# Weighting a pair's sums out of PSUM and adding the six statistics by one matmul in a four-layer graph kernel

## The chip, the cores and the metric

The kernel runs on one core of a Trainium2 chip. The core's engines are TensorE (PE; its weight loads are listed as PEld), VectorE (DVE), ScalarE (ACT), GpSimd (POOL) and SyncE (SP). Here SP issues the transfers between device memory and the on-chip memory SBUF. Matmuls write into PSUM, a small memory of eight banks that VectorE and ScalarE read. The metric is the device time of one execution, in microseconds.

## The reference, cut to what matters

Four graph layers follow each other on 16 graphs of 1024 nodes with 64 channels. The input is x (16, 1024, 64), a 0/1 adjacency adj (16, 1024, 1024) and a node mask. Between the layers stands `x = layernorm(x + layer(x))`. The change touches the first layer. It thins out the neighbours of each node and then takes, for every node and channel, a weighted sum of three quantiles over the values of the node's remaining neighbours:

```python
for tau, wt in zip([0.25, 0.5, 0.75], [0.25, 0.5, 0.25]):
    pos = clip(tau * (mf - 1.0), 0.0)          # mf: number of neighbours left
    lo, hi = floor(pos), ceil(pos)
    frac = pos - lo
    q = gather(lo) * (1 - frac) + gather(hi) * frac   # lo-th and hi-th smallest value
    agg = agg + wt * q
out = x + agg
y = relu(out @ W1 + b1) @ W2 + b2
```

So for each node and channel six values are wanted, the value at `lo` and at `hi` for three quantiles. These are the six statistics (S = 6 in the kernel). Each is multiplied by a weight that depends on the node and the statistic alone (wt times frac or 1 - frac), and the six products are added. Layers 2, 3 and 4 multiply by the adjacency or its transpose: layer 2 three times by adj, layer 3 once by the transposed adjacency with a degree norm, layer 4 once more by it.

## The kernel before, in words

**Steps, units and pairs.** The values of a channel are sorted once. Then for each node the wanted rank is found by counting. Work is cut into units: a graph g, a group gr of eight channels (G8 = 8) and a half h of the nodes (HALF = 512). A unit has six steps, one for each statistic. Two units with the same g and gr, the two halves, make a pair. That gives 96 steps and eight pairs per graph, 128 pairs in all, and 1536 steps. One loop (L1365) runs over the steps y. In each turn it issues, with lags, the parts of several steps at once:

- VectorE: `masks` (L636) of step y+1 and `products` (L644) of step y. A product is written into one of two buffers of the pool `prod`.
- TensorE and ScalarE: `words` (L654) of step y-2 reads a product buffer by matmuls into a bank named pw, and ScalarE copies it out. `ranks` (L666) runs for step y-3 and `steps` (L674) for step y-4. The last ends with the values `val` of a statistic, 8 channels by 512 nodes spread over 128 partitions.
- `Sums.add` (L692) adds `val` of four steps at a time into one PSUM bank, `fc`. After three such adds the bank holds the whole pair: 12 rows of 8 channels, one for each half and statistic, at the partitions that `row_of` (L684) names, by 512 nodes.
- `Sums.store` (L701) runs one turn after the third add: ScalarE copies `fc` into SBUF and SP stores all 128 partitions, 256 KB, to `aggd` in device memory.

TensorE also runs the counting matmuls of the next units (`counts`, L596) and turns the words of the next group into matmul weights (`word_part`, L550). These use two PSUM banks of the tag "y" in turn (`side_bank`, L97): pa, y0, y1 and pw. The weights lie in a pool `wts` of five buffers, two for a group.

**The background.** Beside the steps run generators: the sort of the values for two graphs, the thinning of the next graph's adjacency (`dilate`), the degrees, and the layers of the graph before (`layers`, L830). `Spread` (L977) decides at which half step each generator takes its next step, from a number of steps that is given to it (69 for the layers), a first and a last place, and two running estimates of VectorE's and TensorE's load. Sort steps are fillers: they take places where VectorE's estimate is not ahead. The sorts, the thinning and the degrees are over before the last graphs, which have the steps and the layers alone.

**The order.** `link` (L137) ties the instructions of TensorE, and inside the loop those of VectorE and ScalarE, to the order in which the program issues them. SP's transfers have no such tie and are placed by the framework's scheduler. The SP queue works in order, and each of its transfers can wait for tiles to come free.

**The layers of a graph.** `layers` begins by loading x, the mask, the weights `wd` of the six statistics spread over the channels (three tiles of 128x1024 in 16 bits, six transfers) and the sums from `aggd` (three tiles of 128x1024, twelve transfers). Then VectorE multiplies the three tiles by their weights, adds the three products, and adds the two halves of the result into `pre` (L867 to L875). After that `pre` is scaled, x is added, and the first layer's two matmuls (`ph`, `py`) follow.

**The end.** After the last step only the layers of the last graph are left, one after another. For them `held` (L804) reuses the buffers of the step loop (five of `wts`, two of `cc`, four half buffers of `dw`, four of `prod`, one of `mt`) to hold the whole adjacency and its transpose of the last graph, 16 tiles of 512 KB. It issues the loads in one loop. `stay_warm` (L712) puts matmuls without use into TensorE's order in this part: 72 between the start of the layers and the first `ph`, fewer later.

Of the kernel before, what the change touches and what calls it, by code (L numbers as in the profile page):

```python
# [9 lines left out]
F32 = mybir.dt.float32  # L10
# [9 lines left out]
P = 128  # L20
# [13 lines left out]
S = 6  # L34
# [8 lines left out]
def gnn_stack(  # L43
# [35 lines left out]
    wts = ctx.enter_context(tc.tile_pool(name="wts", bufs=5))  # L79
# [607 lines left out]
    class Sums:  # L687
# [12 lines left out]

        def store(self):  # L701
            v = work.tile([P, HALF], F32, tag="sv", name="v", bufs=1)
            A.copy(v, self.fc)
            nc.sync.dma_start(out=self.gi["aggd"][self.gr], in_=v)
# [99 lines left out]
    def held(g):  # L804

        tiles = []
        for i in range(5):
            t = wts.tile([P, 2, T, P], F16, tag="xw", name="xw").rearrange("p x t m -> p (x t m)")
            tiles.append(t.bitcast(F32))
# [11 lines left out]
        for i in range(1):  # L821
            t = big.tile([P, KC, HALF], F16, tag="mt", name="mt", bufs=6).rearrange("p k n -> p (k n)")
            tiles.append(t.bitcast(F32))
        for j in range(2 * T):
            nc.sync.dma_start(
                out=tiles[j], in_=adj[g, ts(j, P), :] if j < T else adjT[g, ts(j - T, P), :]
            )
        return tiles[0:T], tiles[T : 2 * T]

    def layers(g, aggd, wd, least, den, deg, rows=(), columns=()):  # L830
# [14 lines left out]
        terms, weights = [], []  # L845
        for i in range(S // 2):
            w = wide("w", tag=("hT", "hw", "node")[i]).bitcast(F16)
            w = w.rearrange("p (s n) -> p s n", s=2)
            halves_in(
                w, lambda h: wd[ds(2 * i, 2), ts(h, HALF)].partition_broadcast(C)  # L850
            )
            weights.append(w)
        for i in range(S // 2):
            a = strm.tile([P, N], F32, tag="a", name="v").rearrange("p (s n) -> p s n", s=2)
            for s_ in range(2):
                halves_in(a[:, s_], lambda h: aggd[:, ds(row_of(S * h + 2 * i + s_), G8)])
            terms.append(a)
# [9 lines left out]
        for a, w in zip(terms, weights):  # L867
            yield
            V.tensor_tensor(a, a, w, ALU.mult)
        for a in terms[1:]:  # L870
            yield
            V.tensor_tensor(terms[0], terms[0], a, ALU.add)
        yield
        pre = wide("pre", tag="yT")
        V.tensor_tensor(pre, terms[0][:, 0], terms[0][:, 1], ALU.add)  # L875
# [173 lines left out]
    def info(g):  # L1049
# [14 lines left out]
        nc.sync.dma_start(out=rcs[g % 2][0:S], in_=rd)  # L1064
        infos[g].update(least=least, txw=txw)
# [131 lines left out]


# [306 lines left out]
```

## Time and profile before

| what | value |
|---|---|
| median of 3 runs | 8277.14 us (8274.99 to 8284.68) |
| profiled execution, its own time | 8271.02 us |
| its span in the profile | 8269.2 us |
| first product of the step loop starts at | 297.8 us |
| last product starts at | 8129.1 us |
| one graph of 96 steps | 443 to 513 us |

The profile gives for each engine its busy time and its number of instructions. Groups of instructions are listed by line, engine, operation and tile, with the shape written as partitions x elements, the count, the busy time in us and the mean length in ns. Behind the second bar stands the idle time of the engine just before them and who ended it. A line L176 is the helper that records VectorE's and ScalarE's operations, and L156 the one for matmuls, so the groups are told apart by their tiles: `pr<-mt,dw` is a product, `pw<-pr,red` the matmuls that read it, `fc<-val,fin` the adds, `v<-fc` the copy of `store`, `v<-v,w` the weighting in the layers. A float32 matmul shows as two rows, one for each pass. In the lists of waits a line names the waiting engine and tile, then who ended the wait, and then the total in us, the number of times and the longest. In a timeline the first column is the start and the second the length, both in us. A table by stretch has the stretch and its length, then the busy time and count of PE, PEld, DVE, ACT and POOL, then the granted TensorE clock, the share of the DMA engines and GB/s.

### The profile page before, as it was taken

What the parts mean: (1) busy time and instruction counts of PE and PEld (TensorE: products, weight loads), DVE (VectorE), ACT (ScalarE), POOL (GpSimd) and SP (SyncE); (2) the same over time, 40 slices, a digit from 0 to 9 for tenths busy, and PEclk for the clock granted to TensorE, in tenths of its full rate; (3) what the DMA queues carried; (4) which work ended last, traced back from release to release, by engine and by line L of the source; (5) the groups of instructions that cost most, each with busy time, mean ns of one, the idle gap of its engine ahead of it and who ended that gap; (6) DMA issues with size and microseconds to landing.
All of it is one profiled execution on the core that took longest, in us unless ns stands there. A gap on an engine that the chain in (4) does not pass through costs nothing. (4 is left out here: it accounts for less than half of the span.)

```text
span 8269.2 us, 164242 instructions
## 1 busy us (share of the span) xinstructions
PE 7311.8 (88%) x65169; PEld 2994.8 (36%) x65169; DVE 7826.2 (95%) x8924; ACT 7060.5 (85%) x13562; POOL 1321.6 (16%) x942
## 2 busy tenths in 40 slices
PE   0688889999999899898899999999899999999997
PEld 0233333333333333333333333333333333334333
DVE  9899999999999999999999999999999999887874
ACT  1689889888898889989898898988989888899993
POOL 2210202112021110202112021210202112020000
PEclk9999999999999999999999999999999999999999
DMA  3212222232223232232233322233222233222222
GB/s 101 48 42 53 94 88 93 79 101 98 88 86 87 86 104 91 90 93 90 80 99 104 81 93 89 80 100 94 91 94 85 85 97 104 72 89 72 65 88 68
DMA packets 530453, 711.85 MB, mean 86 GB/s; under 512 B 201488, under 2 KB 328848, under 8 KB 529680
## 3 DMA queue, kind: packets, MB, share of 16 engines
q1 hardware_dynamic: 529680, 701.34, 27.3%
q8 instruction: 510, 8.36, 0.4%
q14 instruction: 263, 2.15, 0.1%
HBM read 602.38 MB, written 98.77 MB: 85 GB/s over the span
## 5 line engine op out<-in xcount | busy, mean ns | idle before, releaser
L176 DVE TENSOR_TENSOR pr<-mt,dw 128x4096 f16<-128x4096 f16 x1536 | 3507.8, 2284 | 222.7 <-PE pw L156 166.7
L156 PE MATMUL x<-vt,xw 128*128 128x512 f16 x8192 | 2317.9, 386 | 0.0
L176 DVE TENSOR_TENSOR mt<-cc,rB 128x2048 f16<-128x2048 f16 x1536 | 1864.7, 1214 | 15.4 <-ACT cc L176 15.4
L176 ACT ACTIVATE pv<-pv,col 128x512 f32<-128x512 f32 x1536 | 1077.1, 701 | 0.0
L156 PEld LDWEIGHTS <-xw 128*128 128x128 f16 x8192 | 737.8, 99 | 819.9 <-issue 298.3
L176 ACT ACTIVATE qq<-pw 128x512 f16<-128x512 f32 x1536 | 962.1, 626 | 16.5 <-PE pw L156 15.9
L156 PE MATMUL pv<-mt,txw 128*32 128x512 f16 x12288 | 951.6, 387 | 8.6 <-ACT pv L176 8.6
L176 ACT ACTIVATE val<-pv 128x512 f32<-128x512 f32 x1536 | 948.9, 618 | 9.2 <-PE pv L156 8.9
L156 PE MATMUL pw<-pr,red 128*32 128x512 f16 x12288 | 937.7, 381 | 14.7 <-DVE pr L176 14.7
L176 ACT ACTIVATE pa<-pa,col 128x512 f32<-128x512 f32 x1020 | 712.5, 699 | 224.8 <-PE pa L156 223.2
L176 ACT ACTIVATE dw<-y 128x512 f16<-128x512 f32 x1024 | 636.9, 622 | 261.2 <-PE y L156 238.7
L734 POOL TENSOR_TENSOR rstd<-var,neghalf 128x8 f32<-128x8 f32 x112 | 250.0, 2232 | 3473.9 <-DVE var L176 3473.9
L176 ACT ACTIVATE cc<-x 128x512 f16<-128x512 f32 x1024 | 620.9, 606 | 190.2 <-PE x L156 112.8
L176 ACT ACTIVATE xw<-pa,col 128x512 f16<-128x512 f32 x1020 | 700.8, 687 | 33.0
L176 ACT ACTIVATE dw<-y,col 128x512 f16<-128x512 f32 x1024 | 719.2, 702 | 1.6 <-PE pv L156 1.1
L156 PE MATMUL pw<-ranks,subr 128*32 128x512 f16 x6144 | 603.0, 382 | 66.5 <-ACT xw L176 64.1
L176 ACT ACTIVATE h<-x 128x512 f16<-128x512 f32 x1024 | 640.0, 625 | 1.0 <-PE x L156 1.0
L176 ACT ACTIVATE l<-x 128x512 f16<-128x512 f32 x1024 | 604.0, 590 | 9.4 <-PE x L156 9.2
L156 PE MATMUL pv<-qq,lead 128*32 128x512 f16 x6144 | 603.6, 381 | 0.0
L156 PE MATMUL x<-h,neg 128*128 128x512 f16 x1024 | 393.9, 385 | 225.3 <-ACT h L176 206.4
L156 PEld LDWEIGHTS <-txw 128*32 128x32 f16 x12288 | 186.3, 94 | 1051.0 <-issue 1050.3
L176 DVE TENSOR_TENSOR sr<-sr 128x384 f16<-128x384 f16 (+9 forms) x1328 | 546.4, 441 | 17.7
(226 smaller groups left out, 10547.6 us busy)
## 6 DMA issues: line engine op xcount, KB each, us to landing
a<-adj_dram SPq DMA_DIRECT2D x360, 512.0 KB
a<-adjT_dram SPq DMA_DIRECT2D x240, 512.0 KB
da<-adj_dram SPq DMA_DIRECT2D x256, 256.0 KB
ac<-adjT_dram SPq DMA_DIRECT2D x256, 256.0 KB
aggd<-v SPq DMA_DIRECT2D x128, 256.0 KB
rB<-rn SPq DMA_DIRECT2D x96, 256.0 KB
v<-aggd SPq DMA_DIRECT2D x192, 128.0 KB
w<-wd SPq DMA_DIRECT2D x96, 128.0 KB
```

The lines of the kernel that those rows point to most:

```text
L156: link("PE", nc.tensor.matmul(out, **kw))
L176: ins = call(*args, **kw)
L734: nc.gpsimd.tensor_tensor(rstd, var, neghalf, ALU.pow)
```

## The change

There are two parts.

**The sums of a pair.** A pair's bank `fc` is no longer copied by ScalarE and stored whole. `weigh` runs on VectorE at the turn where `store` ran: it multiplies the bank by a tile `wf` that holds, at the same partitions, each statistic's weights for the 512 nodes of its half, and writes 128x512 float32 into SBUF. One turn later `store` issues one float32 matmul with a constant 0/1 matrix `choose` (128x32) which adds the six statistics of each half and channel; the result, two blocks of 8 channels, lies in a bank `pu` of the tag "y". ScalarE copies its 32 partitions, and SP stores the two blocks of 16 KB. The two `wf` tiles serve even and odd graphs. They are cleared once, and filled by twelve small transfers per graph at step S+2 of the graph. In `layers` the six weight loads, the twelve loads of sums, the three products and the three sums go; two loads bring `pre`. The layers have 65 steps in `Spread` instead of 69.

**The last graph's adjacency.** `held` takes four buffers of `wts` and two of `mt`, and the pool `wts` has four buffers. It issues the eight loads of the adjacency. The eight of the transposed adjacency are issued by a function that `layers` calls after its load of `pre`.

```diff
-    wts = ctx.enter_context(tc.tile_pool(name="wts", bufs=5))
+    wts = ctx.enter_context(tc.tile_pool(name="wts", bufs=4))
...
+        def weigh(self):
+            self.v = work.tile([P, HALF], F32, tag="sv", name="v", bufs=1)
+            V.tensor_tensor(self.v, self.fc, wfs[self.gi["g"] % 2], ALU.mult)
+
         def store(self):
-            v = work.tile([P, HALF], F32, tag="sv", name="v", bufs=1)
-            A.copy(v, self.fc)
-            nc.sync.dma_start(out=self.gi["aggd"][self.gr], in_=v)
+            pu = side_bank("pu")
+            mm(pu[0:32], choose, self.v, True, True, 0)
+            of = work.tile([32, HALF], F32, tag="of", name="of", bufs=1)
+            A.copy(of, pu[0:32])
+            for h in range(2):
+                nc.sync.dma_start(
+                    out=self.gi["aggd"][h, ds(G8 * self.gr, G8)], in_=of[ds(G8 * h, G8)]
+                )
...
-        for i in range(5):
+        for i in range(4):
             t = wts.tile([P, 2, T, P], F16, tag="xw", name="xw").rearrange("p x t m -> p (x t m)")
...
-        for i in range(1):
+        for i in range(2):
             t = big.tile([P, KC, HALF], F16, tag="mt", name="mt", bufs=6).rearrange("p k n -> p (k n)")
             tiles.append(t.bitcast(F32))
-        for j in range(2 * T):
-            nc.sync.dma_start(
-                out=tiles[j], in_=adj[g, ts(j, P), :] if j < T else adjT[g, ts(j - T, P), :]
-            )
-        return tiles[0:T], tiles[T : 2 * T]
+        for j in range(T):
+            nc.sync.dma_start(out=tiles[j], in_=adj[g, ts(j, P), :])
+
+        def second():
+            for j in range(T):
+                nc.sync.dma_start(out=tiles[T + j], in_=adjT[g, ts(j, P), :])
+
+        return tiles[0:T], tiles[T : 2 * T], second
...
-        terms, weights = [], []
-        for i in range(S // 2):
-            w = wide("w", tag=("hT", "hw", "node")[i]).bitcast(F16)
-            w = w.rearrange("p (s n) -> p s n", s=2)
-            halves_in(
-                w, lambda h: wd[ds(2 * i, 2), ts(h, HALF)].partition_broadcast(C)
-            )
-            weights.append(w)
-        for i in range(S // 2):
-            a = strm.tile([P, N], F32, tag="a", name="v").rearrange("p (s n) -> p s n", s=2)
-            for s_ in range(2):
-                halves_in(a[:, s_], lambda h: aggd[:, ds(row_of(S * h + 2 * i + s_), G8)])
-            terms.append(a)
+        pre = wide("pre", tag="yT")
+        halves_in(pre, lambda h: aggd[h])
+        if load:
+            load()
         yield PE
...
-        for a, w in zip(terms, weights):
-            yield
-            V.tensor_tensor(a, a, w, ALU.mult)
-        for a in terms[1:]:
-            yield
-            V.tensor_tensor(terms[0], terms[0], a, ALU.add)
         yield
-        pre = wide("pre", tag="yT")
-        V.tensor_tensor(pre, terms[0][:, 0], terms[0][:, 1], ALU.add)
         V.tensor_scalar(pre, pre, least[:, 1:2], least[:, 0:1], ALU.mult, ALU.add)
...
+    wfs = []
+    for i in range(2):
+        t = const.tile([P, HALF], F16, name=f"wf{i}")
+        nc.gpsimd.memset(t, 0.0)
+        wfs.append(t)
...
+            pairs_of[w].weigh()
+        w, t = divmod(y - 7, 2 * S)
+        if 0 <= w < n_units // 2 and t == 2 * S - 1:
             pairs_of.pop(w).store()
...
+        if z == S + 2 and g < B:
+            for i in range(2 * S):
+                nc.sync.dma_start(
+                    out=wfs[g % 2][ds(row_of(i), G8)],
+                    in_=infos[g]["wd"][i % S, ts(i // S, HALF)].partition_broadcast(G8),
+                )
...
-                background.append(Spread(after, 69, base + 2 * S, base + 2 * SLOTS - 4))
+                background.append(Spread(after, 65, base + 2 * S, base + 2 * SLOTS - 4))
```

Ten small operations on single columns, left out here, build `choose` at the start.

More of the change, by code (lines that the diff above doesn't have):

```diff
@@ L820, in held, with layers @@
             tiles += [t[:, 0:N], t[:, N : 2 * N]]
-        for i in range(1):
+        for i in range(2):
             t = big.tile([P, KC, HALF], F16, tag="mt", name="mt", bufs=6).rearrange("p k n -> p (k n)")
             tiles.append(t.bitcast(F32))
-        for j in range(2 * T):
-            nc.sync.dma_start(
-                out=tiles[j], in_=adj[g, ts(j, P), :] if j < T else adjT[g, ts(j - T, P), :]
-            )
-        return tiles[0:T], tiles[T : 2 * T]
-    def layers(g, aggd, wd, least, den, deg, rows=(), columns=()):
+        for j in range(T):
[4 more added lines that the diff above has]
+        return tiles[0:T], tiles[T : 2 * T], second
+    def layers(g, aggd, wd, least, den, deg, rows=(), columns=(), load=None):
         V.tensor_tensor(deg[:, 0], deg[:, 0], deg[:, 1], ALU.add)
@@ L1064, in info @@
         nc.sync.dma_start(out=rcs[g % 2][0:S], in_=rd)
+        infos[g]["wd"] = wd
         infos[g].update(least=least, txw=txw)
@@ L1196, in gnn_stack @@
     V.tensor_scalar(fin, iota_w[:, 0:56], fcol, None, ALU.is_equal)
+    choose = const.tile([P, 32], F32, name="choose")
+    eight, place_ = column(21), column(22)
+    V.tensor_scalar(icol[:, 5:6], icol[:, 0:1], 3, None, ALU.logical_shift_right)
+    V.tensor_copy(eight, icol[:, 5:6])
+    V.scalar_tensor_tensor(column(23), eight, -8.0, PCOL, ALU.mult, ALU.add)
+    V.scalar_tensor_tensor(column(24), column(8), -4.0, eight, ALU.mult, ALU.add)
+    V.scalar_tensor_tensor(place_, column(24), 4.0, column(8), ALU.mult, ALU.add)
+    V.tensor_scalar(place_, place_, float(S), float(G8), ALU.is_ge, ALU.mult)
+    V.tensor_tensor(place_, place_, column(23), ALU.add)
+    V.tensor_scalar(column(25), column(24), 3.0, 64.0, ALU.is_ge, ALU.mult)
+    V.tensor_tensor(place_, place_, column(25), ALU.add)
+    V.tensor_scalar(choose, iota_w[:, 0:32], place_, None, ALU.is_equal)
+    wfs = []
[3 more added lines that the diff above has]
+        wfs.append(t)
     second = column(10)
@@ L1370, in gnn_stack @@
         if running and z == 0:
-            infos[g]["aggd"] = dram.tile([G8, P, HALF], F32, name="aggd")
+            infos[g]["aggd"] = dram.tile([2, C, HALF], F32, name="aggd")
             deg = small.tile([P, 3, T], F32, tag="deg", name="deg")
```

## The prediction

> **What bounds the kernel now.** I read the page's busy line first, then busy time by stretch, then who waited for whom, then the groups kept apart by shape, and last the timeline of the end.
>
> ```profile
> PE 7311.8 (88%) x65169; PEld 2994.8 (36%) x65169; DVE 7826.2 (95%) x8924; ACT 7060.5 (85%) x13562; POOL 1321.6 (16%) x942
> ```
>
> VectorE looks like the bound, but the share is an average. By stretch (us, busy time of each engine, granted clock):
>
> ```profile
> 300.00:7090.00 6790.00, 6177.30 (x55401) 2526.72 (x55399) 6695.18 (x7636) 6038.56 (x11585) 1160.09 (x768) 0.98 0.28 87
> 7090.00:8129.00 1039.00, 986.73 (x8966) 399.87 (x8964) 843.49 (x653) 940.55 (x1796) 103.71 (x64) 1.00 0.25 83
> 8129.00:8269.00 140.00, 107.01 (x533) 45.43 (x532) 29.86 (x43) 16.86 (x29) 11.46 (x7) 0.95 0.13 44
> ```
>
> The columns are PE, PEld, DVE, ACT, POOL. Up to 7090 us VectorE is busy 98.6%. From there (the last 24 steps of graph 13, and graphs 14 and 15, with no sort or dilation left) TensorE is busy 95% and VectorE 81%: TensorE sets the pace. The last 140 us are one chain. Inside a graph it also changes. These are pairs (12 steps each) 1, 6 and 7 of graph 11, then 1 and 7 of graph 12:
>
> ```profile
> 5789.00:5850.00 61.00, 52.08 (x467) 21.58 (x465) 60.69 (x60) 55.03 (x107) 18.98 (x11) 0.97 0.19 61
> 6104.00:6169.00 65.00, 63.63 (x609) 26.84 (x598) 61.81 (x73) 56.25 (x107) 1.68 (x1) 1.00 0.36 113
> 6169.00:6224.00 55.00, 53.91 (x479) 21.08 (x481) 53.94 (x54) 49.13 (x93) 2.48 (x1) 1.00 0.42 124
> 6283.00:6343.00 60.00, 52.72 (x443) 21.40 (x440) 59.83 (x58) 54.54 (x106) 17.20 (x10) 0.94 0.18 57
> 6660.00:6722.00 62.00, 56.84 (x485) 22.47 (x487) 58.47 (x71) 49.13 (x92) 2.48 (x1) 0.94 0.37 118
> ```
>
> In pair 1 TensorE has 7 to 9 us to spare; in pairs 6 and 7 of an odd graph it has 1.4 and 1.1, and both engines are full.
>
> ```profile
> DVE pr L176 <- PE pw L156: 166.7, 147, 2.9
> ...
> DVE v L176 <- DMA v<-aggd: 19.0, 3, 17.1
> ```
>
> VectorE's largest wait is for TensorE to free a product buffer. The wait for the sums comes three times, all at the end: the other 15 graphs hide those loads.
>
> **What is removed, and its price.**
>
> ```profile
> L176 DVE TENSOR_TENSOR v<-v,w 128x1024 f32<-128x1024 f32 x48 | 58.4, 1218 | 19.0 <-DMA v<-aggd 19.0
> L176 DVE TENSOR_TENSOR v<-v 128x1024 f32<-128x1024 f32 x32 | 38.9, 1216 | 0.1
> L176 DVE TENSOR_TENSOR x<-pc,rstd 128x512 f32<-128x512 f32 x32 | 21.9, 685 | 13.9 <-POOL rstd L734 13.9
> L176 DVE TENSOR_TENSOR pre<-v 128x512 f32<-128x512 f32 x16 | 10.9, 682 | 0.0
> ...
> L156 PE MATMUL fc<-val,fin 128*32 128x512 f32 x3072 | 401.3, 597 | 0.0
> L156 PE MATMUL po<-msg,wn 128*128 128x512 f32 x32 | 16.3, 592 | 0.0
> L176 ACT COPY v<-fc 128x512 f32<-128x512 f32 x128 | 76.8, 600 | 2.0 <-PE fc L156 2.0
> ```
>
> VectorE instructions overlap by about 0.08 us (below, the 0.68 us op at 8058.48 is followed at 8059.08), so the price is the step from start to start. Per graph that goes: three products and two sums of 128x1024 at 1.22-0.08=1.14 and one 128x512 sum at 0.72, 6.4 us. Added on VectorE: eight weighings of 128x512 out of PSUM per graph. No such op with these operands is shown; rows from PSUM (x<-pc) step by 0.60, from SBUF (pre) by 0.72. I take 0.60, since the operand lies in PSUM: 4.8 per graph; the other end adds about 1 us per graph. So VectorE gains 1.6 us per graph.
>
> Added on TensorE: one float32 128x32x512 matmul per pair, two passes. Bounds: 1.02 (po: 16.3 us over 16) and 1.05 (401.3 us over 384 adds, four column groups side by side). Column groups do not help a lone matmul, so I take 1.05: 8.4 us per graph. ScalarE copies 32 rows instead of 128, the same 512 columns: 0.60 as before.
>
> Waits that the change adds: the weighing waits for the third add. By the trace that add ends 1.3 us or more before VectorE would reach the weighing in all but the last pair: no cost. The matmul waits for the weighing, and TensorE's steps, words and ranks queue behind it. In some 20 of 128 pairs TensorE would reach it early, by 1.5 us at most and 17 us in all, just where TensorE leads VectorE: nothing on the path. The store waits one step longer, and SP's loads behind it with it; VectorE waits for row-rank or adjacency loads nowhere in the list of waits, so a 5 us later issue is covered; uncovered it would show as VectorE waiting on rB or TensorE on a. SP issues 30 transfers a graph instead of 26 (8 stores, 12 and 6 loads become 16 stores, 2 and 12 loads), 14 us of some 490. One weight buffer less: a group's first buffer is needed again 13 half-steps after its last reader, so nothing waits. POOL gets two memsets before the loop.
>
> **What is moved.** The layers have five steps fewer, so the rest of each graph's layers moves forward. I took the built order of the changed kernel's instructions and priced each by its row above or its like. Change per pair 0 to 7, in us. VectorE, odd graphs: +2.7 +5.0 -3.9 +1.1 -2.3 -1.6 -1.6 +2.1 (sum +1.4); even: -1.1 +2.0 -3.9 -0.4 +1.4 +0.4 -0.6 -2.4 (sum -4.6; graph 2 -2.9); graph 0 +4.2 (seven weighings), graph 1 -3.3. TensorE, every graph: +1.1 +7.9 -1.2 +0.1 -1.3 +4.4 -0.7 -1.8 (sum +8.4). Sort steps fill what the layers leave, which is why odd graphs get none of the gain.
>
> **The sum**, stretch by stretch:
> - Start: ten small ops, +0.7. Graph 0 +4.2. Graph 1 -3.
> - Even graphs 2 to 12 (six): VectorE alone gives -25.9. TensorE's +7.9 in pair 1 meets 7.3 us of idle time and is then level with VectorE; I let 1.5 us of each gain go: -18.
> - Odd graphs 3 to 11 (five): VectorE +2.6 over pairs 0 to 4. Pairs 5 to 7 are between -1.1 (VectorE) and +1.9 (TensorE), nearer the fuller TensorE: +1.4. So +4 each, +20. Graph 13 to step 72, +3.
> - From 7090: TensorE -2.5 (pairs 6, 7 of graph 13) +8.4 +7.4 = +13. VectorE's gains are worth nothing there.
> - The end, -2.5:
>
> ```profile
> 8058.48 0.68 DVE L176 TENSOR_TENSOR x<-pc,rstd 128x512 f32<-128x512 f32 x1
> 8059.08 1.22 DVE L176 TENSOR_TENSOR mt<-cc,rB 128x2048 f16<-128x2048 f16 x1
> ...
> 8157.37 0.55 DVE L176 TENSOR_SCALAR pre<-pre,least 128x512 f32<-128x512 f32 x1
> ```
> ```profile
> 8135.97 2.86 PE L156 MATMUL fc<-val,fin 128*32 128x512 f32 x8
> ...
> 8138.94 16.04 PE L156 MATMUL warm<-ranks,ident 128*128 128x512 f16 x72
> 8158.79 1.10 PE L156 MATMUL ph<-pre,w 128*128 128x512 f32 x2 [3.81 <-DVE pre L176]
> ```
>
> Sums ready at 8138.9. New chain: weighing 0.7, matmul 1.05 to 2.1 (the adds before it took 2.86 instead of 1.05, granted clock 0.66), copy 0.6, store to first load 2.65 as before, two loads instead of twelve (4 us instead of 15), two ops 1.3: ready near 8150 instead of 8158.6. But the 72 warming matmuls stand behind the new matmul and ahead of ph, and take 16: ph starts near 8157, gain 1.7. With no idle time ahead, the second ph and py may keep the higher clock (2.08 and 1.98 now), so -2.5; ends +0.5 and -4.6. The later load is later in the text alone: in the built SP order all eight transposed loads still stand before the last stores: 0. Nothing needs them before 8232.
>
> The Trainium skill, "TensorE: Matmul & The Clock Gate", Part 1, says the array runs at half clock after an idle window of about 3.4 us; by it the lone matmul costs 2.1 us here and ph, py and pc save some 2.9: the end would be -4. "DMA: Bandwidth & Descriptors", Rules for kernel authors, says transfers under 64 KB are mostly overhead and should be joined, which speaks against two 16 KB stores for one of 256 KB: at its fixed 2 us that would be an estimated +2 on the end and nothing where 25 us lie between store and use.
>
> Sum: 0.7+4.2-3-18+20+3+13-2.5 = +17. The profiled execution took 8271.0 (span 8269.2), so 8288 against it; it is 6 us under the median 8277.1, so the median goes to 8294.
>
> **The rivals.**
> 1. TensorE absorbs all that is moved to it before 7090; VectorE's sums stand: 0.7+4.2-3.3-25.9+7+1+13-2.5 = -6, 8271. For: 8% of idle TensorE time. Against: much of it is waiting on ScalarE (h 206 us), which returns. Chance 0.20.
> 2. The other side, faster: as 1, and pairs 6 and 7 of odd graphs end with TensorE, whose work there falls by 2.5 where VectorE's rises by 0.5. Six graphs at -3: 8253. It decides if pair 5's 4.6 us of idle time takes its +4.4. Chance 0.10.
> 3. Moved TensorE work is not covered: half of 8.4 in graphs 1 to 12 comes on top of rival 1, +50: about 8322. For: VectorE's products find their buffer less than 1.1 us free in 30% of the steps. Chance 0.23.
> 4. The load of the sums is late and stalls VectorE, 2 us in 15 graphs, +30: 8307. Against: six steps, 25 us or more, lie between the last store and the use, and the chain is about 11. Chance 0.03.
>
> **How the numbers follow.** Forecast 8294, own range 8284 to 8306, 0.44. A 0.2% difference is 16.5 us, about what a measurement of this kernel can tell. The forecast lies on that line: half slower, half same. Rivals 3 and 4 are slower, 1 same, 2 faster: 0.10 faster, 0.42 same, 0.48 slower. Range: 8264, between rivals 1 and 2, to 8326, rival 3 with 4 us of the dearer weighing; that leaves out most of rival 2 and the upper part of 3.
>
> **What would show it.** Weighing 0.68 us long x128; pu 256 passes, about 135 us busy; stretch after 7090 longer by some 13; even graphs shorter by 3, odd longer by 4; ph right after the warming with no idle time; v<-aggd waits gone, none on pre but at the end. Wrong if VectorE's wait for pw before 7090 grows by more than 40 us (rival 3) or if odd graphs shrink (rival 2).

## The result, and the profile after

The changed kernel takes 8333.67 us (median of 4 runs, 8330.97 to 8343.42), the kernel before 8277.53 in the same comparison. The ratio is 1.0068, interval 1.0055 to 1.0080: slower by 56 us. The forecast was 8294 us, with a range from 8264 to 8326. The profiled execution has a span of 8329.2 us, 60.0 more than before.

The page of the changed kernel, busy time of each engine:

```profile
PE 7422.2 (89%) x65425; PEld 3049.8 (37%) x65425; DVE 7813.4 (94%) x8966; ACT 7075.2 (85%) x13562; POOL 1210.9 (15%) x944
```

VectorE has 12.8 us less work than before and the kernel is 60 us longer. So VectorE did not get more work; it stands idle more. The table by stretch (columns as in the prediction; the borders are the start of the steps, step 72 of graph 13 and the last product):

```profile
301.00:7163.00 6862.00, 6286.15 (x55668) 2578.31 (x55670) 6693.73 (x7672) 6056.63 (x11594) 1058.55 (x768) 0.98 0.26 79
7163.00:8195.00 1032.00, 993.18 (x8967) 405.42 (x8963) 838.71 (x655) 939.02 (x1791) 93.71 (x64) 1.00 0.22 72
8195.00:8329.00 134.00, 103.32 (x535) 43.96 (x527) 23.37 (x37) 16.78 (x28) 11.45 (x7) 1.00 0.11 38
```

The same step took place at 7092.7 us before and at 7162.9 now. The whole loss lies before it (+70); the last two and a quarter graphs are 4.6 us shorter, the end 5.7. The mean granted clock of TensorE is 0.984 in both executions. VectorE's list of waits says what it waits for:

```profile
DVE pr L176 <- PE pw L156: 188.1, 175, 3.4
...
DVE yn L176 <- POOL rstd L743: 29.4, 17, 1.8
DVE x L176 <- POOL rstd L743: 22.5, 13, 2.1
DVE pr L176 <- ACT of L176: 20.6, 11, 2.9
DVE sr L176 <- DMA ac<-adjT_dram: 18.9, 6, 3.8
```

Here pr is a product, sr a tile of the sort, and x, yn and xn are the multiplications by rstd of the different layers. In the kernel before, the second and third line read 14.5 and 13.9, and the fifth was not there:

```profile
DVE yn L176 <- POOL rstd L734: 14.5, 8, 1.8
DVE x L176 <- POOL rstd L734: 13.9, 12, 1.8
```

All rows of this list added up, by the work that waits (us; "rstd" is every wait for GpSimd's rstd, "sort" the waits of the sort's tiles sr, m and sv, "others" mostly the start and the end):

| kernel | products (pr) | rstd | sort | others | sum | VectorE busy |
|---|---|---|---|---|---|---|
| before | 221.3 | 28.4 | 11.9 | 122.9 | 384.5 | 7826.2 |
| after | 250.3 | 53.7 | 30.0 | 119.3 | 453.3 | 7813.4 |

68.8 of waits less 12.8 of work makes 56.0 of the 60.0 us. Products wait 29 us longer, the multiplications by rstd 25, the sort 18.

The even graphs 2 to 12 and the odd graphs 3 to 11 do not lose in the same way. Sums over them, changed kernel against the kernel before (us; gaps too short for the list of waits are left out):

| graphs | length | VectorE work | products | rstd | sort |
|---|---|---|---|---|---|
| six even | +27.0 | -20.3 | +6.6 | +19.7 | +16.3 |
| five odd | +31.1 | +10.2 | +16.1 | +5.9 | +0.2 |

The waits sit in a few places that repeat from graph to graph. In pair 3 yn waits 1.7 us for rstd in twelve of the graphs 1 to 13, which it did in none of them before. Another place is pair 6 of the even graphs, which costs 7.7 us more than before in graph 4 (pair 7 behind it takes 5.1 less). VectorE's timeline there, changed kernel:

```profile
2697.91 2.29 DVE L176 TENSOR_TENSOR pr<-mt,dw 128x4096 f16<-128x4096 f16 x1 [1.50 <-PE pw L156]
...
2703.18 2.29 DVE L176 TENSOR_TENSOR pr<-mt,dw 128x4096 f16<-128x4096 f16 x1 [1.18 <-PE pw L156]
...
2706.11 1.23 DVE L176 TENSOR_TENSOR sv<-sv 128x1024 f16<-128x1024 f32 x1
...
2709.26 2.29 DVE L176 TENSOR_TENSOR pr<-mt,dw 128x4096 f16<-128x4096 f16 x1 [0.79 <-PE pw L156]
...
2712.18 0.17 DVE L176 TENSOR_SCALAR var<-var 128x8 f32<-128x8 f32 x1
2714.17 0.69 DVE L176 TENSOR_TENSOR x<-pc,rstd 128x512 f32<-128x512 f32 x1 [1.82 <-POOL rstd L743]
...
2721.30 0.69 DVE L176 CAST sr<-ii 128x1024 f16<-128x1024 int32 x1 [3.11 <-DMA ac<-adjT_dram]
```

And the same work in the kernel before:

```profile
2676.21 1.23 DVE L176 TENSOR_TENSOR sv<-sv 128x1024 f16<-128x1024 f32 x1
...
2690.91 0.69 DVE L176 CAST sr<-ii 128x1024 f16<-128x1024 int32 x1 [0.36 <-issue]
...
2702.95 0.17 DVE L176 TENSOR_SCALAR var<-var 128x8 f32<-128x8 f32 x1
2703.03 0.42 DVE L176 TENSOR_TENSOR sr<-sr 128x508 f16<-128x508 f16 x1
2703.48 0.42 DVE L176 TENSOR_TENSOR sr<-sr,m 128x508 f16<-128x508 f16 x1
2703.93 1.21 DVE L176 TENSOR_TENSOR sr<-sr 128x508 f16<-128x508 f16 x3
2705.06 0.68 DVE L176 TENSOR_TENSOR x<-pc,rstd 128x512 f32<-128x512 f32 x1
```

This is the largest single place of waiting. A layer's normalization goes var, then rstd on GpSimd, then x. Before, three sort rows (five operations) stood between var and x, and x found rstd ready. Now the sort hands over from one run of sorting (sv) to the next (sr<-ii) just when the normalization comes. Nothing stands between var and x, VectorE waits 1.82 us, and the new run (sr<-ii) starts behind it and waits 3.11 more, which the profile puts down to a DMA; the eight transfers that store the last run stand in SP's queue just before (issued from 2706.74 to 2716.68). sr and sv are buffers of one pool, so the new run can be waiting for those stores: in the kernel before too it started 4.4 us behind the issue of the last of them, but there VectorE had other work until then. No VectorE instruction got dearer. Two background streams met.

Not everything came out worse. The new operations cost what they were priced at (groups of the changed kernel):

```profile
L156 PE MATMUL pu<-v,choose 128*32 128x512 f32 x256 | 138.9, 626 | 28.7 <-DVE v L176 28.3
...
L176 DVE TENSOR_TENSOR v<-fc,wf 128x512 f32<-128x512 f32 x128 | 87.3, 682 | 6.6 <-PE fc L156 6.6
```

And at the end the chain is as forecast, only faster (TensorE's timeline, changed kernel):

```profile
8204.36 1.04 PE L156 MATMUL pu<-v,choose 128*32 128x512 f32 x2 [0.79 <-DVE v L176]
...
8205.46 15.93 PE L156 MATMUL warm<-ranks,ident 128*128 128x512 f16 x72
8221.25 1.10 PE L156 MATMUL ph<-pre,w 128*128 128x512 f32 x2
8223.13 1.12 PE L156 MATMUL ph<-pre,w 128*128 128x512 f32 x2 [0.78 <-ACT hid L176]
```

The first ph follows the warming with no idle time, and the second ph takes 1.12 instead of 2.08.

### The profile page after: what moved, and what is told of

It reads as the page before. It is cut to its first block, busy times and chain, and to the rows that moved or that the text cites. A ratio compares the mean times of both kernels' runs of the same rounds, so it can differ in the third digit from the quotient of the medians.

```text
span 8329.2 us, 164826 instructions
## 1 busy us (share of the span) xinstructions
PE 7422.2 (89%) x65425; PEld 3049.8 (37%) x65425; DVE 7813.4 (94%) x8966; ACT 7075.2 (85%) x13562; POOL 1210.9 (15%) x944
## 4 chain that ended last, share of the span: by engine, by line
DVE 26%; PE 26%; ACT 15%; issue 8%; POOL 2%; DMA 1%; SPq 0%; POOLq 0%; DVEq 0%; ACTq 0%
DVE pr L176 9%; PE x L156 8%; DVE mt L176 6%; PE pa L156 4%; DVE sr L176 4%; PE pv L156 4%; PE pw L156 4%; ACT dw L176 3%; PE y L156 2%; ACT h L176 2%; ACT val L176 2%; DVE sv L176 2%; PE fc L156 2%; DVE sc L176 2%; DVE vt L176 1%
## 5 line engine op out<-in xcount | busy, mean ns | idle before, releaser
L176 DVE TENSOR_TENSOR pr<-mt,dw 128x4096 f16<-128x4096 f16 x1536 | 3509.1, 2285 | 252.7 <-PE pw L156 188.1
L156 PE MATMUL pv<-mt,txw 128*32 128x512 f16 x12288 | 1030.4, 387 | 7.7 <-ACT pv L176 7.7
L156 PE MATMUL pw<-pr,red 128*32 128x512 f16 x12288 | 983.6, 380 | 48.8 <-DVE pr L176 48.7
L156 PE MATMUL pw<-ranks,subr 128*32 128x512 f16 x6144 | 645.9, 382 | 69.2 <-ACT xw L176 59.1
L743 POOL TENSOR_TENSOR rstd<-var,neghalf 128x8 f32<-128x8 f32 x112 | 231.5, 2067 | 3262.3 <-DVE var L176 3262.3
L156 PE MATMUL pv<-qq,lead 128*32 128x512 f16 x6144 | 643.6, 380 | 0.0
L176 ACT ACTIVATE l<-x 128x512 f16<-128x512 f32 x1024 | 603.7, 590 | 11.5 <-PE x L156 11.1
L156 PEld LDWEIGHTS <-txw 128*32 128x32 f16 x12288 | 211.0, 94 | 913.2 <-issue 911.9
L451 POOL TENSOR_SCALAR sk<-sc 128x1 f32<-128x1 f16 x128 | 122.5, 957 | 2890.6 <-DVE sc L176 1852.8
```

The lines of the kernel that those rows point to most:

```text
L156: link("PE", nc.tensor.matmul(out, **kw))
L176: ins = call(*args, **kw)
L451: G.tensor_scalar(sk[:, 0:1], m, 0.5, 0.5, ALU.add, ALU.mult)
L743: nc.gpsimd.tensor_tensor(rstd, var, neghalf, ALU.pow)
```

## The experiments

The first four runs set two theories against each other. **A**: the loss comes from the layers' background steps, which stand elsewhere when five of them go. **B**: it comes from the added matmul on TensorE. The later ones ask what in A costs. Times are medians; the kernel before had medians of 8276.5 to 8278.6 in these comparisons.

### Undoing one part

**The steps' places given back.** The changed kernel with five empty steps ahead of the scaling of `pre`, and the old pace.

```diff
-        yield
+        for _ in range(6):
+            yield
...
-                background.append(Spread(after, 65, base + 2 * S, base + 2 * SLOTS - 4))
+                background.append(Spread(after, 69, base + 2 * S, base + 2 * SLOTS - 4))
```

> The changed kernel whole, with five empty steps put into the layers where the three products and the two sums stood, and 69 steps as before; so the layers' later steps and the sort steps go back to the places they had. Theory A (the time comes from the background's steps that moved forward, not from the new operations): graph 0 about +4 us, graphs 1 to 13 between -2 and 0 each, the last two graphs -4 to 0, the end -5.6 and the start +3.3 as in the changed kernel: about 8262 us, 8250 to 8275. Theory B (the new matmul on TensorE and the wait it makes cost some 5 us in every graph, wherever the layers stand): about 8325 to 8335.

8288.76 us, ratio 1.0014 (1.0005 to 1.0023). 45 of the 56 us are gone: mostly A, though above its range, with a rest of 11. Waits of the sort fall from 30.0 to 10.5, those for rstd only to 48.9.

**The move alone.** The kernel before with its six VectorE steps of weighting joined to one, pace 65.

```diff
+        yield
         for a, w in zip(terms, weights):
-            yield
             V.tensor_tensor(a, a, w, ALU.mult)
         for a in terms[1:]:
-            yield
             V.tensor_tensor(terms[0], terms[0], a, ALU.add)
-        yield
         pre = wide("pre", tag="yT")
...
-                background.append(Spread(after, 69, base + 2 * S, base + 2 * SLOTS - 4))
+                background.append(Spread(after, 65, base + 2 * S, base + 2 * SLOTS - 4))
```

> The kernel before, nothing of the change in it, but with the layers' six VectorE steps on the sums joined into one step and 65 steps instead of 69, so that the layers' later steps move forward as in the changed kernel. No operation is added or left out. Theory A: slower by 40 to 60 us, graphs 2 to 12 longer by some 4 each, and the even graphs' seventh pair longer by about 8. Theory B: within 10 us of before.

8374.67 us, 1.0115 (1.0099 to 1.0132). The loss is larger than in the changed kernel, since six operations in one place are a burst that the changed kernel does not have (pair 0 is 5.9 us longer in even graphs, 8.5 in odd). It supports A in sign; its size says nothing.

**The later loads alone.** The kernel before with the second part of the change.

```diff
-        for j in range(2 * T):
-            nc.sync.dma_start(
-                out=tiles[j], in_=adj[g, ts(j, P), :] if j < T else adjT[g, ts(j - T, P), :]
-            )
-        return tiles[0:T], tiles[T : 2 * T]
+        for j in range(T):
+            nc.sync.dma_start(out=tiles[j], in_=adj[g, ts(j, P), :])
+
+        def second():
+            for j in range(T):
+                nc.sync.dma_start(out=tiles[T + j], in_=adjT[g, ts(j, P), :])
+
+        return tiles[0:T], tiles[T : 2 * T], second
```

> The kernel before with only the second part of the change: the eight loads of the last graph's transposed adjacency are issued from inside the layers, after the loads of the sums. Both theories: the scheduler still puts them before the last store, so 8277, within 5 us.

8277.88 us, 0.9999 (0.9990 to 1.0009): nothing, as forecast.

**The matmul alone.** The kernel before with one float32 matmul of 128x32x512 more per pair, which nothing reads.

```diff
+            self.v = v
+
+        def extra(self):
+            mm(side_bank("pu")[0:32], fin[:, 0:32], self.v, True, True, 0)
```

> The kernel before with one more float32 128x32x512 matmul for each pair, one step after the copy of the pair's sums, from that copy into a bank of the tag y; nothing reads its result. Everything else as before. TensorE gets 1.05 us per pair, 134 us in all. Theory A: 0 to 10 us slower, since idle TensorE time takes it. Theory B: 40 to 60 us slower. My prediction's term for the last two graphs and a quarter, where TensorE is busy 95%, was 13 us for this matmul: if that holds, these graphs alone are longer by 15 to 17.

8315.04 us, 1.0045 (1.0030 to 1.0060): 37 us, against A's 0 to 10 and just under B's 40 to 60. But TensorE's time is not all that changed: the planner counts the matmul, so sort steps moved on VectorE too (its waits for rstd rose from 28.4 to 41.1). From step 72 of graph 13 to the last product, where no sort is left, the run is 14.9 us longer than before.

**The same matmul in 16 bits.**

```diff
-            mm(side_bank("pu")[0:32], fin[:, 0:32], self.v, True, True, 0)
+            mm(side_bank("pu")[0:32], ident16[:, 0:32], rcs[self.gi["g"] % 2][:, 0:HALF], True, True, 0)
```

> The kernel before with one matmul more per pair, into a side bank, that nothing reads, as in the matmul-alone run (8315.0 us, 37 us over the kernel before), but in 16 bits: one pass of 0.22 us in place of two passes, 1.05 us. It reads the ranks' columns instead of the stored sums, so it waits for nothing new. Theory T (TensorE's time on the path): 37 x 0.22/1.05 = 8, so 8285 us (8280 to 8291). Theory B (the turn in the side banks): 8312 (8305 to 8318). The two 16-bit runs so far gained 14.6 us with the places back and nothing in the changed kernel, where T had 28.

8285.23 us, 1.0011 (1.0002 to 1.0021): 8 us, theory T's number. The turn in the side banks alone is not what costs. Here VectorE's work per pair stands as in the kernel before in all but three pairs of graph 1 (nine pairs differ in the run in float32), so this is the cleaner of the two. It is not the same matmul in everything else: it reads the ranks' columns and so waits for no copy.

### What in the order costs

**Warming ahead of pm.** In the place shown above TensorE waits 2.13 us, to 2690.16, for VectorE before `pm`, and the granted clock (third number from the end) then falls, to half for 6.83 us:

```profile
2686.00:2692.00 6.00, 3.87 (x91) 2.48 (x84) 6.00 (x5) 3.03 (x6) 0.00 (x0) 0.85 0.06 12
2692.00:2698.00 6.00, 6.00 (x36) 1.81 (x33) 4.25 (x12) 3.55 (x8) 0.00 (x0) 0.58 0.15 44
2690.16:2696.99 6.83, 6.83 (x82) 3.33 (x86) 6.00 (x12) 2.85 (x6) 0.00 (x0) 0.50 0.11 30
```

The run adds matmuls without use there:

```diff
         pm = bank(ps_l, "pm")
+        for _ in range(24):
+            link("PE", nc.tensor.matmul(
+                pm[:, 0:P], lhsT=ident16, rhs=ident16, start=True, stop=True,
+                skip_group_check=True,
+            ))
```

> The changed kernel (8333.7 us) with 24 matmuls of 128 columns without use into pm's bank, just ahead of the 64 matmuls with one column each that fill pm; VectorE's and ScalarE's orders and the places of all steps stay as they are. In graph 4 of the changed kernel TensorE waits 2.13 us there for VectorE, the granted clock falls to 0.58 for some 6 us, and VectorE then waits 1.50 + 1.18 + 0.79 us for words. Theory C (the fallen clock makes the words late): the clock stays at 0.9 or more there, the three waits fall under 0.5 us in all, even graphs are 3 us shorter: 8313 us (8306 to 8320). Theory L (the words are late because of the 64 matmuls and the wait ahead of them): the waits stay, 8334 (8330 to 8342), more if the 24 matmuls, some 2 us, don't fit into the wait.

8345.45 us, 1.0083 (1.0068 to 1.0098). In the same two stretches of this run the clock stays up:

```profile
2686.00:2692.00 6.00, 3.77 (x46) 1.93 (x46) 6.00 (x6) 3.79 (x7) 0.00 (x0) 1.00 0.06 14
2692.00:2698.00 6.00, 6.00 (x107) 3.60 (x105) 5.51 (x13) 3.27 (x8) 0.00 (x0) 1.00 0.05 15
```

The first wait of VectorE falls from 1.50 to 0.25 us; the other two stay at 1.19 and 0.80. The time is theory L's, but this run can't price the clock: its 24 matmuls start only when VectorE's result is there (behind the same 2.12 us of waiting) and put 1.50 us of their own ahead of the words. The changed kernel itself holds a better comparison. In its graph 10 the same `pm` stands behind the same 2.13 us of waiting, but the clock did not fall:

```profile
5690.50:5697.00 6.50, 6.35 (x101) 3.65 (x102) 6.26 (x14) 3.90 (x9) 0.00 (x0) 1.00 0.12 40
```
```profile
5701.10 2.29 DVE L176 TENSOR_TENSOR pr<-mt,dw 128x4096 f16<-128x4096 f16 x1 [0.20 <-PE pw L156]
...
5707.18 2.29 DVE L176 TENSOR_TENSOR pr<-mt,dw 128x4096 f16<-128x4096 f16 x1 [0.79 <-PE pw L156]
```

There VectorE's first wait is gone, the second is 0.20 instead of 1.18, and the third stays. Graph 10 is 2.3 us longer than before, graphs 4, 6, 8 and 12, where the clock fell, 5.0 to 5.6. So the clock explains the first wait and most of the second, some 3 us in a graph, as theory C had it. The waits for rstd and of the sort are there in graph 10 too (1.82 and 3.13 us).

**rstd half a step later.** The changed kernel, in which x keeps two half steps of distance from var instead of one, so that other VectorE work comes in between.

```diff
-        yield KEEP
+        yield KEEP + "2"
         dst = wide(name, tag="node")
...
-                return place >= self.held + (2 if "p" in self.next else 1)
+                return place >= self.held + (2 if "p" in self.next or "2" in self.next else 1)
```

> The changed kernel (8333.7 us) in which the multiplication by rstd keeps one half step more of distance from the variance, so that other VectorE work stands between them in nearly all places (places with nothing between fall from 18 to 7). Of 112 places the changed kernel waits at 30 for GpSimd's rstd, 51.9 us in all; the kernel before waits 28.4. Theory W (these waits are time on VectorE's path): the waits fall to 15 us or less and the time by 25 to 40 us, to 8301 us (8293 to 8310). Theory M (where the layers' bundle of TensorE work falls is what counts, and a wait that goes comes back as a wait for words): the waits for rstd fall, those for pw rise by as much, and the time stays within 10 us of 8333.7.

8300.71 us, 1.0029 (1.0018 to 1.0041): 33 us gained, theory W's 8301. All waits for rstd fall from 53.7 to 14.1, those of the sort from 30.0 to 11.4; those of the products rise from 250.3 to 283.6. Pair 6 of graph 4 goes from 7.7 us over the kernel before to 0.7 under it, and the even graphs 4 to 12 end 1.8 to 2.5 us shorter than before. The gain lies in the even graphs: the odd graphs 3 to 11, 31.1 us over the kernel before in the changed kernel, are 38.2 over it here, though no wait for rstd of more than 0.2 us is left in them.

**The same edit on the kernel before and on the places-back kernel.** First on the kernel before:

> The kernel before (8277 us) with the half step more between the variance and the multiplication by rstd, and nothing else. It waits 28.4 us in all for GpSimd's rstd, at 20 places. Theory W (those waits are time on VectorE's path): they go and the time falls by 15 to 25 us, to 8257 us (8250 to 8265). Theory M (the gain of this edit on the changed kernel, 33 us, came from another place for the layers' TensorE work, and the kernel before has none to gain): 8277 (8270 to 8285).

8272.74 us, 0.9994 (0.9984 to 1.0003): 4 us, inside theory M's range and not W's. The waits for rstd fall from 28.4 to 12.7 here too, and those for product buffers rise by 19. In this order a wait that goes comes back as another. Then on the places-back kernel:

> The places-back kernel (8288.8 us, in float32 as the changed kernel) with the half step more ahead of the multiplication by rstd. It waits 47.1 us in all for rstd, at 26 places. Theory W: 30 to 40 us go, to 8254 us (8246 to 8264), which is below the kernel before. Theory M: 8286 (8278 to 8294).

8266.19 us, 0.9988 (0.9978 to 0.9997): 23 us less than the places-back kernel, short of the 30 to 40 expected, since products wait 14 us longer. With the change and in float32, it is 10 us faster than the kernel before, and 6.5 us faster than the kernel before with the same half step.

**The pace alone.** The changed kernel, pace 69 for its 65 steps, nothing else.

```diff
-                background.append(Spread(after, 65, base + 2 * S, base + 2 * SLOTS - 4))
+                background.append(Spread(after, 69, base + 2 * S, base + 2 * SLOTS - 4))
```

> The changed kernel with the layers' pace of before, 69 steps for 65 that there are, and no empty step: every step of the layers comes earlier still than in the changed kernel, up to five steps at the end. The built order has a multiplication by rstd directly behind its variance in 10 places instead of 18. Theory W (waits for rstd are most of what the moved steps cost): those waits fall to about 30 us and the time to 8310 us (8300 to 8320). Theory P (the steps' places themselves, early or late against the other work, are what costs): no better than the changed kernel, 8330 us or more.

8267.04 us, 0.9986 (0.9976 to 0.9995). One number, the planner's count of steps, takes off 67 us, far more than either theory gave it. The instructions and their number are the same, the waits of the products too (250.3 and 252.4); those for rstd and of the sort fall by 56.5 of the 65.2 us by which the span is shorter. VectorE's waits in this run:

```profile
DVE pr L176 <- PE pw L156: 185.4, 172, 3.1
...
DVE yn L176 <- POOL rstd L743: 12.4, 7, 1.8
```

**Empty steps, pace 65.** The places-back kernel with the changed kernel's pace.

```diff
-                background.append(Spread(after, 69, base + 2 * S, base + 2 * SLOTS - 4))
+                background.append(Spread(after, 65, base + 2 * S, base + 2 * SLOTS - 4))
```

> The changed kernel with the five empty steps ahead of the scaling but with the pace of 65 steps for now 70: the last steps are late and come in a bundle where they are due. The built order has a multiplication by rstd directly behind its variance in 41 places instead of 18. Theory W: the waits for rstd rise to 75 us or more and the time stays high, 8325 us (8310 to 8345), though TensorE's added work lies within 1.6 us of even in all pairs but the last. Theory P (TensorE's bundles decide): 8295 us (8285 to 8305), near the places-back kernel's 8288.8.

8367.35 us, 1.0106 (1.0091 to 1.0121): theory W's side, but 22 us above its range. The waits for rstd are up to 77.4 us in all, those of the sort to 43.4, though by the built order TensorE's work lies more evenly than in the changed kernel.

```profile
DVE yn L176 <- POOL rstd L743: 40.7, 23, 1.8
DVE pr L176 <- ACT of L176: 38.1, 23, 3.5
DVE x L176 <- POOL rstd L743: 34.9, 20, 1.8
DVE sr L176 <- DMA wd<-sc: 18.4, 3, 6.2
```

**Pace 73**, on the changed kernel:

```diff
-                background.append(Spread(after, 65, base + 2 * S, base + 2 * SLOTS - 4))
+                background.append(Spread(after, 73, base + 2 * S, base + 2 * SLOTS - 4))
```

> The changed kernel with a pace of 73 steps for the layers (65: 8333.7 us; 69: 8267.0 us). The built order has 14 multiplications by rstd directly behind their variance (18 with 65, 10 with 69); TensorE's work in pair 1 is the same as with 69, 9.8 us over the kernel before. If the time goes with the waits for rstd it lies between the two, nearer 69: 8285 us (8270 to 8300). If a quicker pace is better in itself: below 8267 us.

8269.64 us, 0.9990 (0.9980 to 0.9999), between the two expectations. Rstd and sort waits are as high as 38.0 and 38.6, but products wait only 190.9: another order, and nearly the time of pace 69.

**The control: the kernel before at another pace.**

```diff
-                background.append(Spread(after, 69, base + 2 * S, base + 2 * SLOTS - 4))
+                background.append(Spread(after, 73, base + 2 * S, base + 2 * SLOTS - 4))
```

> The kernel before (8277 us) with a pace for the layers of 73 steps for its 69 or 70, and nothing else: the control for the run with 69 steps for the changed kernel's 65. Theory Q (the quicker pace helps any of these kernels): 8250 us (8240 to 8260). Theory S (the kernel before has few waits for rstd, 28.4 us, of which removing all gained 4 us, so there is little for another pace to gain): 8277 us (8268 to 8290).

8333.75 us, 1.0067 (1.0052 to 1.0082). Both theories were wrong. Without any of the change, another pace costs the kernel before as much as the change did, by other waits: the sort's are up from 11.9 to 47.7 us, most of it one kind that the kernel before had for 3.6.

```profile
DVE pr L176 <- PE pw L156: 161.2, 149, 3.4
...
DVE pr L176 <- ACT xw L176: 44.9, 35, 2.6
DVE m L176 <- DMA sv<-xT_dram: 29.2, 7, 5.2
```

The account of VectorE's waits and work (us, profiled executions, made as the table above) closes to within 4 us for all of them:

| kernel | median | products | rstd | sort | others | waits and work, to before | span, to before |
|---|---|---|---|---|---|---|---|
| after | 8333.7 | 250.3 | 53.7 | 30.0 | 119.3 | +56.0 | +60.0 |
| places back | 8288.8 | 234.6 | 48.9 | 10.5 | 124.3 | +14.2 | +14.3 |
| rstd later | 8300.7 | 283.6 | 14.1 | 11.4 | 122.7 | +29.3 | +31.0 |
| pace 69 | 8267.0 | 252.4 | 19.6 | 7.6 | 123.9 | -4.2 | -5.2 |
| empty steps, pace 65 | 8367.4 | 232.2 | 77.4 | 43.4 | 143.5 | +96.1 | +96.2 |
| pace 73 | 8269.6 | 190.9 | 38.0 | 38.6 | 139.2 | -5.5 | -7.6 |
| before, pace 73 | 8333.8 | 234.6 | 25.2 | 47.7 | 129.1 | +56.5 | +57.7 |

### The shorter matmul

If the matmul costs, a shorter one should gain. Five runs have v and choose in 16 bits, so that the matmul is one pass and the sums are rounded to 16 bits before they are added.

```diff
-            self.v = work.tile([P, HALF], F32, tag="sv", name="v", bufs=1)
+            self.v = work.tile([P, HALF], F16, tag="sv", name="v", bufs=1)
...
-    choose = const.tile([P, 32], F32, name="choose")
+    choose = const.tile([P, 32], F16, name="choose")
```

On the places-back kernel:

> The kernel of the places-back run (six empty steps ahead of the scaling, 69 steps; 8288.8 us), with the weighing's result v and the 0/1 matrix choose in 16 bits, so that the matmul is one pass. One pass of 512 columns in 16 bits takes 0.22 us here (the 72 warming matmuls took 15.93 us) against 1.05 for the two passes in float32. Theory T (the 37 us that the matmul alone cost are TensorE's time): 0.79 of it goes, 29 us, so 8260 us (8252 to 8270), below the kernel before. Theory B (the cost is the turn taken in the two side banks and the copy out of them, whatever the matmul's length): 8287 (8282 to 8293). The weighing's own length should stay near 0.68 us; if it falls, that part is to be taken off first. The sums are rounded to 16 bits before they are added.

8274.17 us, 0.9998 (0.9989 to 1.0007): 14.6 us less than in float32, half of theory T's 29. The weighing kept its 0.68 us.

On the changed kernel:

> The changed kernel (8333.7 us) with v and choose in 16 bits and nothing else. Theory T: 8333.7 - 29 = 8305 us (8297 to 8315). Theory B: 8331 (8326 to 8337). If the two costs, the matmul and the moved steps, are independent, this run stands as far under the changed kernel as the 16-bit run with the places back stands under its own float32 form, within 6 us.

8337.78 us, 1.0069 (1.0053 to 1.0086): nothing gained. Theory B's time came out, but the 16-bit matmul alone speaks against the turn in the side banks as its reason (the copy out of the bank was in neither of those two runs); the costs are not independent.

On the places-back kernel with rstd half a step later:

> The same on the places-back kernel with the weighted sums and the 0/1 matrix in 16 bits (8274.2 us, 47.1 us of waits for rstd in it too). Theory W: 8240 us (8231 to 8252). Theory M: 8272 (8264 to 8280).

8243.79 us, 0.9961 (0.9948 to 0.9975): the fastest of all, 33 us under the kernel before, and near theory W's 8240.

On the changed kernel with rstd half a step later:

> The changed kernel with the half step more ahead of the multiplication by rstd (8300.7 us) and with the weighted sums and the 0/1 matrix in 16 bits. In 16 bits the changed kernel gained nothing (8337.8 after 8333.7), the places-back kernel 14.6 us, and with rstd later 22.4 us. Theory H (the waits for rstd hid the shorter matmul: VectorE stood at rstd however early TensorE was): now it gains too, 15 to 28 us: 8280 us (8272 to 8287). Theory N (in the order of the changed kernel TensorE's own bunches decide, with or without rstd): 8300 us (8294 to 8307).

8313.55 us, 1.0042 (1.0028 to 1.0057): 13 us slower than in float32. Neither theory had that; so it was not the waits for rstd that hid the gain.

On the changed kernel at pace 69:

> The changed kernel with the layers' pace of 69 steps (8267.0 us, waits for rstd 17.8 us), with the weighted sums and the 0/1 matrix in 16 bits. Theory H (where VectorE does not wait for rstd, a shorter matmul is time): 15 to 25 us less, 8248 us (8240 to 8256). Theory N (in the changed order, without the places given back, TensorE's shorter work gains nothing, as in the two runs of that kind): 8267 us or more.

8262.98 us, 0.9980 (0.9970 to 0.9989): 4 us gained, between the theories.

So the same shorter matmul is worth 22, 15, 4, -4 and -13 us in five orders. Part of this is that the planner counts a 16-bit matmul as a quarter, so VectorE's built order differs between float32 and 16 bits in every one of the five pairs. How much of each number is TensorE's time and how much is the order stays open.

## Why the prediction was wrong

By its own stretches (us, profiled executions, a stretch from the first product of a graph to that of the next):

| stretch | forecast | measured |
|---|---|---|
| start | +0.7 | +3.3 |
| graph 0 | +4.2 | +3.7 |
| graph 1 | -3 | -0.4 |
| even graphs 2 to 12 | -18 | +26.9 |
| odd graphs 3 to 11 | +20 | +31.1 |
| graph 13 to step 72 | +3 | +5.5 |
| graph 13 from step 72, 14, 15 | +13 | -4.6 |
| the end | -2.5 | -5.7 |
| sum | +17 | +60 |

**Right.** The prices of the instructions: the weighing 682 ns long, 128 of them; the new matmul 138.9 us busy, forecast some 135. The weighing waits for nothing but the last add (6.6 us, once). The waits on v<-aggd went; pre waits once, at the end (6.42 us). Graph 0, and in the odd graphs the work by the built order: in graph 5 the first three pairs measure +2.4, +4.3 and -4.0 against +2.7, +5.0 and -3.9. That the odd graphs' sum comes within 11 us of the forecast is in part luck: only 10.2 of their 31.1 us are work, and 5.9 are waits for rstd, which the forecast did not have. The second part is worth nothing. At the end ph follows the warming and keeps the clock, as the Trainium skill, "TensorE: Matmul & The Clock Gate", Part 1, would have it for an array without a long idle window; the end fell by 5.7 where its rule gave 4 and I took 2.5. The 2.1 us that the rule gave the lone matmul did not come: it took 1.04, with the clock at 1.00 there. Inside the loop the clock fell behind a shorter wait than that page's 3.4 us, 2.13 (last section); there the measurement counts. The two small stores, against which "DMA: Bandwidth & Descriptors", Rules for kernel authors, was weighed, caused no wait on `pre` in 15 of the 16 graphs.

**The step that failed: even graphs.** "VectorE alone gives -25.9 ... I let 1.5 us of each gain go: -18" priced what moves by its work alone, and let only TensorE's fullness take some back. (The terms as given there add up to -16.9.) The work came near: -20.3. But the moved normalization met the sort's hand-over, and over the six graphs the waits for rstd grew by 19.7 us, those of the sort by 16.3 and those of the products by 6.6 (VectorE's gaps over 0.3 us, mean of graphs 4, 6, 8 and 12: 3.8 us before, 11.5 after). The page of before had the lines: `x<-pc,rstd` waiting 13.9 us for GpSimd stood in the prediction as a price row, and its wait was passed over. The run with rstd half a step later gives even graphs 4 to 12 the -3 that was forecast, nearly (-1.8 to -2.5). This step missed by 45 us; the whole sum missed by 43, since the other misses cancel.

**The step that failed the other way: from step 72 of graph 13.** Forecast was that TensorE is the bound there and +13 come on top. TensorE's busy time did rise, from 983.8 to 993.2 us, yet the stretch got shorter: its idle time fell from 52 to 39 us. 9 us of that is one kind of wait, for ScalarE. TensorE's list of waits in this stretch, kernel before:

```profile
PE x L156 <- ACT h L176: 23.3, 37, 1.7
```

Changed kernel:

```profile
PE x L156 <- ACT h L176: 14.0, 29, 1.7
```

An engine that is busy 95% of a stretch still had room, and the order decided how much of it was used. With the matmul alone the stretch is 14.9 us longer than before, near the forecast; with the places given back it is 7.8 longer, and with pace 69 it is 5.8 shorter.

**The waits that the change adds** were put at 17 us, none on the path. The wait of the new matmul for v measures 28.3 us; that it reached the path was not shown.

**The rivals.** Rival 3, moved TensorE work that is not covered, 8322, was nearest in size. Its sign of recognition, VectorE's wait for pw before 7090 growing by more than 40 us, did not come, though more of it came than the sum over the whole kernel shows (166.7 to 188.1). Kernel before, from the first product to that step, and changed kernel, to the same step:

```profile
DVE pr L176 <- PE pw L156: 24.0, 36, 2.4
```
```profile
DVE pr L176 <- PE pw L156: 55.5, 67, 2.9
```

That is 31.5 us more. Rival 3 charged half of 8.4 us per graph in graphs 1 to 12; with the float32 matmul alone these graphs are 24 us longer, about half of that charge, and that with the order moved too. The matmul in 16 bits costs 8 us in all. So part of rival 3 is real, but the waits for rstd and of the sort, more than half of what VectorE waits longer before that step (46 of 69 us), were named by none of the rivals. The forecast's likeliest sign, slower, held, but not for its reasons: of its +17 the last graphs were to give 13, and they gave -4.6.

**What stays open.** Why, order by order, the waits come out as they do: the account closes, but no rule was found that gives it beforehand. The number of multiplications directly behind their variance does not give it: 18 in the changed kernel, 14 in the kernel at pace 73, which is 64 us faster. What makes the odd graphs 31 us longer was not found either: taking their waits for rstd away did not shorten them. Every run at pace 65 took 8300 us or more, every run at 69 but the matmul alone 8289 or less; whether 65 is a bad number for any of these kernels is open, for the kernel before was not run at it with its own steps. That the sort's 3.1 us wait is for the store of the run before was read from SP's queue and not tried alone.

## What to carry to other kernels

Where background work is woven into a full engine by a planner, a change that removes steps moves all later ones, and the planner's own step count is a knob of the same size as the change: 65, 69 and 73 gave 8334, 8267 and 8270 us with the same instructions, and the untouched kernel lost 56 us between 69 and 73. So compare a change at its best pace, not at one, and run the kernel before at another pace as the control before a cause is put to the edit. When pricing a move, list every cross-engine hand-over among the moved steps (here var, rstd, x, 1.8 us when nothing lies between) and look at what will stand between its two ends; then take that distance out of the planner's hands, as the half step more did. It gained 33, 23 and 4 us in three orders, so it too has to be tried in the order at hand.

## What was not expected of the hardware

- GpSimd's rstd on 128x8 values, a handful of numbers, holds VectorE for 1.82 us from the end of var to the start of x when nothing else is there to do (group mean on GpSimd 2.07 us). It cost nothing where sort work filled the 1.94 us between them (graph 4 of the kernel before).
- The granted clock fell to 0.50 for 6.83 us when a wait of 2.13 us ended (graph 4 of the changed kernel), before the 64 matmuls of a single column behind it had run. After the same wait in graph 10 of the same run, with the same 64 matmuls, it stayed at 1.00. What decides between the two was not tried. In the kernel before the wait there is 0.42 us, and the stretch around it shows 1.00.
- One float32 matmul per pair whose result nobody reads cost 37 us, of 134 us that it takes at 1.05 us each (and an order that moved with it); in 16 bits, reading other data, 8.
